# The v projection of an attention block as a sixth pair of seven products, turned to tokens afterwards

## The chip, the cores and the metric

The kernel runs on one core of one Trainium2 chip. The metric is the device time of one execution, in microseconds (us). All arithmetic is in 32-bit floats.

## The reference, cut to what matters

The input x has 32 sequences of 64 tokens with 1024 features. Two blocks follow each other, each with a residual: attention on a projection of x that carries a low-rank addition per sequence, and a feed-forward part with two stages of low-rank experts. Only the attention is touched here:

```
c   = x @ W.T + 0.5 * (x @ lora_A[label]) @ lora_B.T      # per sequence, rank 32
qkv = c @ w_qkv.T + b_qkv                                 # 1024 q, 256 k, 256 v columns
q, k, v = split(qkv)         # 32 query heads, 8 key/value heads of 32
q, k = rope(q), rope(k)
s   = q @ k.T / sqrt(32), causal within the 64 tokens
x   = x + (softmax(s) @ v) @ w_o.T + b_o
```

## The kernel before, in words

The 2048 tokens are taken in two halves of 1024 (the loop over `hf`, which begins at line 897). Ahead of the loop the weights are multiplied out once: `cqkv` is w_qkv times W, so that q, k and v come from x in one product, and `b1q` holds the matching low-rank rows. x lies with features on the partitions (eight tiles of 128 x 1024).

*A pair by seven products.* Large products are made as 2x2 blocks by seven block products in place of eight (class `Group`, lines 231 to 339). A pair is 256 output features. `weight_sums` (line 172) makes four sums of its weights on GpSimd, lines 179 to 182; `column_sums` (line 185) makes four sums of the right side on VectorE, lines 191 to 197. The sums of x, `xt`, are made once per half in four tiles of 128 x 4 x 512, `sum0` to `sum3` (`all_column_sums`, line 224). A step, for example `p1`, is four matmuls of 128 x 128 by 512 columns, all recorded at line 261: p1 uses the plain weights and x, p5 uses weight sum 1 and `sum0`, p6 weight sum 2 and `sum1`, p7 weight sum 3 and `sum2`, p4 `sum3`, p3 weight sum 4, p2 plain operands. p6 and p7 end in a VectorE addition (lines 288 and 300), p1 in a ScalarE copy (line 282). `RankGroup` (line 375) adds the low-rank rows as matmuls with 32 contraction rows (line 385), [...]; the row of the last block is held back to the next pair (`last_rows`, `held`).

*q and k* are five such pairs (`qk_pair`, line 950). Their results get bias and rope: a shuffle, two products and a sum, on VectorE and GpSimd (lines 937 to 948).

*v* is made otherwise. For each of eight blocks of 128 tokens, `v_mult` (line 988) runs eight matmuls with a block of x as the stationary side and 256 columns of weights as the moving side, so that v comes out with tokens on the partitions, as the softmax needs it. `v_ranks` (line 975) adds the low-rank rows at line 979 and `v_out` (line 999) the bias. The weights are loaded by `load_w` at the end of the fifth pair.

*Softmax by units.* A unit is four sequences of one group of four key/value heads; there are eight units in a half. `scores` (1004) makes four banks of scores on TensorE; `masked` (1030) adds the mask on VectorE into tiles `e`; `maxima` (1039) takes the row maxima on VectorE and subtracts them on GpSimd (line 1044); `normalised` (1046) takes exponentials on ScalarE (1048), sums and reciprocals on VectorE (1053, 1054) and multiplies on GpSimd (1056); `turned` (1058) transposes each `e` on TensorE into a bank `pt` (line 1064) and copies it on ScalarE to `ws` (1066); `values` (1070) multiplies with v (1079) and copies two banks to q's place on ScalarE (1087). Banks come from two rings of PSUM: five of `ps_tile`, three of `group_bank`.

*The order* of the stage is written out by hand (`with tc.manual_schedule()` from line 1177), on all engines: every engine takes its instructions in the order in which the program names them. Units 0 and 1 begin in the last two q pairs. Then, in the stage around the change (lines 1212 to 1233):

```
for u in range(4):
    ws = turned(u)
    if u > 0: normalised(u + 1)
    v_mult(2u+1); v_out; masked(u + 2)
    v_ranks; v_mult(2u+2); maxima(u + 2); v_out
    values(u, ws)
```

so each unit's values follow its transposes after one or two v products. The column sums of the output projection, `o_sums` (line 1131), are made from two units at a time on VectorE between them. Units 4 to 7 are then worked between the steps of the output projection's pairs (lines 1239 to 1269).

Of the kernel before, what the change touches and what calls it, by code (L numbers as in the profile page):

```python
# [13 lines left out]
F32 = mybir.dt.float32  # L14
# [5 lines left out]
P = 128  # L20
D = 1024
KC = D // P
B, S = 32, 64
T = B * S
HD, NH, NKV = 32, 32, 8
# [15 lines left out]
for _name, _w in (  # L41
    ("ident", P),
    ("cos", S),
    ("sin", S),
    ("mask", S),
    ("parts", 2 * E),
    ("stack", P),
    ("em8", E),
    ("row", 1),
    ("biases", 10 + 2 * KC),  # L50
    ("bv", NKV * HD),
):
    _C[_name] = slice(_n, _n + _w)
    _n += _w
# [22 lines left out]
def block_kernel(ctx: ExitStack, tc: tile.TileContext, a, out: bass.AP):  # L77
# [32 lines left out]
    em8, row = cst[:, _C["em8"]], cst[:, _C["row"]]  # L110
    biases, bv = cst[:, _C["biases"]], cst[:, _C["bv"]]

# [20 lines left out]
    for n in (512, 512, 128):  # L133
        nc.tensor.matmul(ps[:, :n], idle[:, :P], idle[:, :n], start=True, stop=True)
    bqk, bo, bb = biases[:, 0:10], biases[:, 10 : 10 + KC], biases[:, 10 + KC :]

# [87 lines left out]
    def all_column_sums(name, pool, b, n):  # L224
        t = columns(name, pool, b, n)
        for j in range(4):
            for kc in range(H):
                t.make(kc, (j,))
        return t
# [145 lines left out]
    class RankGroup(Group):  # L375
# [22 lines left out]
        def together(self, held=None):  # L398
# [6 lines left out]
            if held is not None:  # L405
                held.out01()

        def p4(self):
            self.mult(self.y, "22", "t4")
            self.out(1, 0, self.y, self.add10)  # L410
# [85 lines left out]
    b1q = const.tile([P, NQ], F32, tag="b1q", name="b1q")  # L496
    b1d = const.tile([P, 5, P], F32, tag="b1d", name="b1d")
    b2s = scratch.tile([P, NF], F32, tag="b2s", name="b2s")
# [7 lines left out]
    with tc.tile_pool(name="gen", bufs=1) as gen:  # L506
# [190 lines left out]
        make_cf(1, 2, 3)  # L697
        differences(b1d, b1q, 5)
        b2 = hp.tile([P, TH], F32, tag="hw", name="b2").rearrange("p (k o) -> p k o", o=P)
# [197 lines left out]
    for hf in range(2):  # L897
# [13 lines left out]
        attention, pools = pools, ExitStack()  # L911
        xt = all_column_sums(f"x{hf}", scoped(f"sums_x{hf}"), x_half, 512)
        if hf == 0:
            low = first_pass["low"]
        else:
            low = new_low(hf)
            a1 = q[:, 1].rearrange("p b m t -> p b (m t)")
            tiles = [a1[:, s * BS : (s + 1) * BS] for s in range(NS)]
            steps = [ranks(hf, s, x, tiles[s : s + 1], low) for s in range(NS)]
            first_halves, second_halves, sums = zip(*steps)  # L920
# [29 lines left out]
        def qk_pair(g, z_bank=group_bank):  # L950
# [4 lines left out]
            def out(r, c, ps, add):  # L955
                oc = 2 * g + r
                raw = tmp(f"raw_{hf}_{oc}_{c}")
                bias = bqk[:, oc : oc + 1]
                if add is None:
                    nc.scalar.activation(raw, ps, AF.Identity, bias=bias)  # L960
                else:
                    nc.vector.scalar_tensor_tensor(raw, ps, bias, add, ALU.add, ALU.add)
                rope(oc, c, raw)

# [5 lines left out]

        begun = {}

        def v_ranks(*ts):
            for at, t in enumerate(ts):
                begun[t] = group_bank(f"v_{hf}_{t}")[:, :WG]
                rows = slice(at * LR, (at + 1) * LR)
                nc.tensor.matmul(
                    begun[t],  # L980
                    low[rows, t * P : (t + 1) * P],
                    b1q[rows, 5 * WG :],
                    start=True,
                    stop=False,
                    skip_group_check=True,
                )

        def v_mult(t):
            for kc in range(KC):
                nc.tensor.matmul(  # L990
                    begun[t],
                    x[kc][:, t * P : (t + 1) * P],
                    wv[:, kc, :],
                    start=False,
                    stop=kc == KC - 1,
                    skip_group_check=True,
                )

        def v_out(t):
            nc.vector.tensor_add(v[:, t, :], begun.pop(t), bv)  # L1000

        def scores(u):
            g, b0 = u // 4, u % 4 * 4
            sc = [ps_tile(f"sc_{hf}_{u}_{j}") for j in range(4)]
            for n in range(8):
                mp, b = n // 4, b0 + n % 4
                for j in range(4):
# [47 lines left out]

        def turned(u):

            turned = []  # L1060
            for j, e in enumerate(units.pop(u)):
                pt = ps_tile(f"pt_{hf}_{u}_{j}")
                for n in range(4):
                    nc.tensor.transpose(pt[:, n * P : (n + 1) * P], e[:, n * P : (n + 1) * P], ident)  # L1064
                ws = wsp.tile([P, 512], F32, tag="ws", name=f"ws_{hf}_{u}_{j}")
                nc.scalar.copy(ws, pt)  # L1066
                turned.append(ws)
            return turned

        def values(u, turned, bank=ps_tile):  # L1070
# [3 lines left out]
            for i in range(2):  # L1074
                for j in range(4):
                    for b in range(2):
# [3 lines left out]
                            av[b][j * HD : (j + 1) * HD, i * 256 : (i + 1) * 256],  # L1080
                            v[rows, b0 // 2 + i, head * HD : (head + 1) * HD],
                            turned[j][rows].rearrange("p (m i q) -> p i m q", m=2, i=2)[:, i],
# [3 lines left out]
            for b in range(2):  # L1086
                nc.scalar.copy(
                    q[:, g, b0 + b : b0 + 4 : 2, :, :],
                    av[b].rearrange("p (i m t) -> p i m t", i=2, t=S),
                )  # L1090
# [86 lines left out]
        with tc.manual_schedule():  # L1177
# [3 lines left out]
            for u in range(2):  # L1181
# [16 lines left out]
                else:  # L1198
                    wv = load_w(cqkv[:, :, 5 * WG :], f"v{hf}")
                g.p4()  # L1200
                g.p3()
            g.last_rows()
            v_ranks(0, 1)
            g.out01()
            v_mult(0)
            rotated()
            pools.close()
            wsp = scoped(f"ws{hf}", 4)
            sums = scoped(f"sums_o{hf}")
            t0 = [sums.tile([P, 2, 512], F32, tag=f"sum{j}", name=f"sum{j}_o{hf}0") for j in range(4)]  # L1210
            v_out(0)
            for u in range(4):
                first, second = 2 * u + 1, 2 * u + 2
                ws = turned(u)
                if u > 0:
                    normalised(u + 1)
                v_mult(first)
                v_out(first)
                if 0 < u < 3:
                    o_sums(0, t0, u - 1, u)  # L1220
                masked(u + 2)
                if u == 3:
                    values(u, ws, group_bank)
                    o_sums(0, t0, u - 1, u + 1)
                    maxima(u + 2)
                    break
                v_ranks(second, second + 1)
                v_mult(second)
                maxima(u + 2)
                v_out(second)  # L1230
                values(u, ws)
                if u == 0:
                    wo0 = o_load(0, 0)

            wo1 = o_load(0, 1)
# [3 lines left out]
            for u in range(4, 8):  # L1239
                o = pairs[u - 4]  # L1240
                ws = turned(u)
                o.p1()
# [377 lines left out]
```

## Time and profile before

| what | before |
|---|---|
| three runs | 1198.10, 1198.75, 1201.41 us; median 1198.75 |
| the profiled execution | 1199.29 us, its span 1197.5 us |
| busy in the span | TensorE 1186.4 us, VectorE 695.5, GpSimd 533.5, ScalarE 156.9 |
| v products (line 990) | 256 records, 382 ns each, 58.7 us busy |
| transposes of the units (line 1064) | 256 records, 274 ns each, 31.0 us busy |
| the stage around the change, first half | 429.44 to 482.39 us: TensorE busy 52.95, VectorE 47.2, GpSimd 30.4, ScalarE 19.5 |

The span is the time from the first to the last recorded instruction; the profiled execution's own time is 1.8 us more. PE is TensorE, DVE is VectorE, ACT is ScalarE, POOL is GpSimd, SP is the engine that issues most DMAs, PEld is TensorE's loading of weights. A matmul of 32-bit floats appears as two records, a transpose as one. Matmuls are pipelined, so the duration of one record is longer than the distance to the next; what a group costs is the distance from its start to the start of the next group. In a timeline a row gives start and duration, line, operation, written and read tiles, and in brackets the idle time before it with what released it.

### The profile page before, as it was taken

How to read it: one execution, taken by the hardware profiler on the slowest of the kernel's cores; microseconds unless marked ns; L12 is line 12 of the kernel's file. 1: busy time of each engine (PE TensorE's matmuls, PEld its weight loads, DVE VectorE, ACT ScalarE, POOL GpSimd, SP SyncE). 2: the span in 40 equal slices, each digit the busy share in tenths (PEclk: the TensorE clock that was granted, in tenths of full speed). 3: DMA queues.
4: the chain of work that ended last, by engine and by line, in shares of the span. 5: the costliest groups of instructions: out<-in, count | busy, mean ns of one | idle time of the engine just before them, and what ended most of it. 6: DMA issues, size and time to landing. Idle time of an engine off the chain costs nothing.

```text
span 1197.5 us, 15158 instructions
## 1 busy us (share of the span) xinstructions
PE 1186.4 (99%) x5916; PEld 703.9 (59%) x5916; DVE 695.5 (58%) x1221; ACT 156.9 (13%) x302; POOL 533.5 (45%) x477
## 2 busy tenths in 40 slices
PE   9999999999999999999999999999999999999998
PEld 3444874555444468544458887444468644458887
DVE  4313151619556798764757554555898774657552
ACT  1000100000000214330011000000114430011000
POOL 3341355242442756662804533543756762812231
PEclk9999999999999999999999999999999999999999
DMA  6652754858311120122217665111120222313543
GB/s 246 214 216 87 260 176 145 284 165 285 93 35 36 36 71 4 69 71 83 91 36 217 188 201 180 37 35 36 36 71 2 71 71 71 104 31 108 156 145 102
DMA packets 114679, 136.71 MB, mean 114 GB/s; under 512 B 6576, under 2 KB 92976, under 8 KB 113328
## 3 DMA queue, kind: packets, MB, share of 16 engines
q1 hardware_dynamic: 101120, 111.52, 29.2%
q10 hardware_dynamic: 10800, 15.84, 3.7%
q0 software_dynamic: 2688, 8.39, 2.0%
q8 instruction: 47, 0.77, 0.3%
q14 instruction: 24, 0.20, 0.0%
HBM read 101.02 MB, written 34.71 MB: 113 GB/s over the span
## 4 chain that ended last, share of the span: by engine, by line
PE 98%; DMA 1%; SPq 0%; issue 0%; DVE 0%; ACT 0%
PE qk_y L261 9%; PE o_y L261 7%; PE f_y L261 6%; PE qk_x L261 6%; PE qk_z L261 6%; PE v L990 5%; PE o_x L261 5%; PE o_z L261 5%; PE f_x L261 4%; PE f_z L261 4%; PE cf_y L261 3%; PE cq_y L261 3%; PE sc L1011 3%; PE pt L1064 2%; PE cq_z L261 2%; PE f_z L273 2%
## 5 line engine op out<-in xcount | busy, mean ns | idle before, releaser
L938 POOL TENSOR_TENSOR raw<-raw,consts 128x512 f32<-128x512 f32 x40 | 63.1, 1585 | 104.6 <-DVE t L937 104.6
L1044 POOL TENSOR_TENSOR e<-e,top 128x512 f32<-128x512 f32 x64 | 65.0, 1045 | 57.2 <-DVE top L1043 42.2
L261 PE MATMUL f_y<-s_f,w_f 128*128 128x256 f32 x336 | 82.2, 380 | 0.5 <-DVE f_u L300 0.5
L1056 POOL TENSOR_TENSOR e<-e,tot 128x512 f32<-128x512 f32 x64 | 66.2, 1066 | 27.3 <-DVE tot L1054 27.3
L261 PE MATMUL qk_x<-x,w_qk 128*128 128x512 f32 x160 | 72.5, 595 | 0.7 <-ACT qk_p L282 0.7
L261 PE MATMUL qk_y<-sum_x,s_qk 128*128 128x512 f32 x160 | 72.2, 594 | 0.0
L261 PEld LDWEIGHTS f_y<-s_f,w_f 128*128 128x128 f32 x336 | 63.7, 190 | 9.6 <-DVE f_u L300 0.9
L261 PE MATMUL o_x<-q,w_o 128*128 128x512 f32 x128 | 58.9, 592 | 0.0
L990 PE MATMUL v<-w_v,x 128*128 128x256 f32 x256 | 58.7, 382 | 0.0
L1171 POOL TENSOR_TENSOR x<-x,o_u 128x512 f32<-128x512 f32 x24 | 30.9, 1291 | 54.5 <-DVE o_u L1169 33.2
L261 PEld LDWEIGHTS qk_x<-x,w_qk 128*128 128x128 f32 x160 | 30.1, 190 | 39.5 <-issue 37.9
L990 PEld LDWEIGHTS v<-w_v,x 128*128 128x128 f32 x256 | 47.4, 190 | 8.4 <-issue 2.7
L261 PEld LDWEIGHTS qk_y<-sum_x,s_qk 128*128 128x128 f32 x160 | 30.2, 190 | 37.1 <-issue 36.4
L939 DVE TENSOR_TENSOR t<-t,consts 128x512 f32<-128x512 f32 x40 | 48.7, 1229 | 0.7
L1053 DVE TENSOR_REDUCE tot<-e 128x8 f32<-128x512 f32 x64 | 40.5, 667 | 10.7 <-ACT e L1048 10.4
L1048 ACT ACTIVATE e<-e 128x512 f32<-128x512 f32 x64 | 38.3, 641 | 54.2 <-POOL e L1044 54.2
L1034 DVE TENSOR_TENSOR e<-sc,consts 128x512 f32<-128x512 f32 x64 | 39.7, 677 | 8.8 <-PE sc L1011 8.8
L948 DVE TENSOR_TENSOR q<-raw,t 128x512 f32<-128x512 f32 x32 | 38.4, 1206 | 2.5 <-POOL raw L938 2.3
L1043 DVE TENSOR_REDUCE top<-e 128x8 f32<-128x512 f32 x64 | 39.6, 675 | 0.0
L261 PEld LDWEIGHTS o_x<-q,w_o 128*128 128x128 f32 x128 | 23.7, 190 | 26.8 <-issue 26.8
L1066 ACT COPY ws<-pt 128x512 f32<-128x512 f32 x64 | 33.0, 612 | 41.8 <-PE pt L1064 41.8
L261 PE MATMUL qk_y<-sum_x,w_qk 128*128 128x512 f32 x80 | 37.0, 605 | 0.0
(364 smaller groups left out, 2376.1 us busy)
## 6 DMA issues: line engine op xcount, KB each, us to landing
w_f<-cf SPq DMA_DIRECT2D x28, 512.0 KB, 4.0
w_f<-cf SPq DMA_DIRECT2D x28, 384.0 KB, 7.4
w_qk<-cqkv SPq DMA_DIRECT2D x10, 1024.0 KB, 6.7
x<-in_xT SPq DMA_DIRECT2D x16, 512.0 KB, 7.7
w_o<-in_wo SPq DMA_DIRECT2D x16, 512.0 KB
s_o<-wos SPq DMA_DIRECT2D x16, 512.0 KB, 6.6
outT<-o ACTq DMA_DIRECT2D x20, 256.0 KB, 4.0
cqkv<-cq ACTq DMA_DIRECT2D x16, 256.0 KB, 2.3
```

Source lines behind the costliest of these rows:

```text
L261: self.last = nc.tensor.matmul(ps, self.weights[left][:, kc, :], self.right(right, kc), start=first and kc == 0, stop=kc == self.h - 1, sk ...
L938: nc.gpsimd.tensor_mul(rv, rv, c3)
L939: nc.vector.tensor_mul(t2v, t2v, s3)
L948: nc.vector.tensor_add(*unfinished.pop())
L990: nc.tensor.matmul(begun[t], x[kc][:, t * P : (t + 1) * P], wv[:, kc, :], start=False, stop=kc == KC - 1, skip_group_check=True,)
L1011: nc.tensor.matmul(sc[j][:, n * S : (n + 1) * S], q[rows, g, b, 2 * mp : 2 * mp + 2, :].rearrange("p m t -> p (m t)"), k[rows, g, b, :], s ...
L1034: nc.vector.tensor_add(per_key(e), per_key(sc[j]), mask.unsqueeze(1).to_broadcast([P, 8, S]))
L1043: nc.vector.tensor_reduce(top, ev, AX.X, ALU.max)
L1044: nc.gpsimd.tensor_sub(ev, ev, wide(top))
L1048: nc.scalar.activation(e, e, AF.Exp, scale=SCALE)
L1053: nc.vector.tensor_reduce(tot[:, i], es[i], AX.X, ALU.add)
L1056: nc.gpsimd.tensor_mul(es[i], es[i], wide(tot[:, i]))
```

## The change

v becomes a sixth pair of the same form (`qk_pair(5)`): seven products of 512 columns with four weight sums on GpSimd, using the same sums of x. Its results come with features on the partitions, get their bias from a column of `bqkv`, skip the rope and wait in four tiles `v_blocks`. `v_turned` transposes them to tokens with eight TensorE transposes for each half of the columns, and ScalarE copies the banks to `v`. The order of the tokens in v differs from before, so `scores` takes its sequences in the order 0, 2, 1, 3 and `values` reads v at another place.

The `ws` tiles and the tiles of the output projection's sums no longer have pools of their own: they stand in the places of `sum0` to `sum3` whose last product has run (`in_place_of`). The hand-written order changes: p1 and p5 of the v pair come first, units 0 to 3 are turned between its steps, and the values of units 0 to 3 come in a row after it, when v is complete. `normalised(4)` stands after the values of unit 1 and the first `o_sums`. The fifth unit's masks stand ahead of the values. The constants lose the 256 columns of v's bias, and `b1d` gets a sixth block. The core of the diff:

```diff
-        def v_ranks(*ts):
...
-        def v_mult(t):
...
-        def v_out(t):
...
+        def some(self, *what, held=None):
+
+            for at, (r, c) in enumerate(what):
+                self.rows(self.z if c == 1 else self.y if r == 1 else self.x, r, c, at)
+            if held is not None:
+                held.last_rows()
...
+        def in_place_of(j, name):
+
+            return xt.pool.tile([P, 4, 512], F32, tag=f"sum{j - 1}", name=f"{name}_{hf}")
...
-                rope(oc, c, raw)
+                if g == 5:
+                    v_blocks[r, c] = raw
+                else:
+                    rope(oc, c, raw)
...
+        v_blocks = {}
+
+        def v_turned(c):
+            for two in range(2):
+                ps = group_bank(f"v_{hf}_{c}_{two}")
+                for n in range(4):
+                    i, r = 2 * two + n // 2, n % 2
+                    nc.tensor.transpose(
+                        ps[:, n * P : (n + 1) * P], v_blocks[r, c][:, i * P : (i + 1) * P], ident
+                    )
+                at = 4 * c + 2 * two
+                nc.scalar.copy(v[:, at : at + 2, :].rearrange("p t o -> p (t o)"), ps)
...
+        ORDER = (0, 2, 1, 3)
...
-                mp, b = n // 4, b0 + n % 4
+                mp, b = n // 4, b0 + ORDER[n % 4]
...
-                ws = wsp.tile([P, 512], F32, tag="ws", name=f"ws_{hf}_{u}_{j}")
+                ws = to[:, j]
...
-                            v[rows, b0 // 2 + i, head * HD : (head + 1) * HD],
+                            v[rows, 4 * i + b0 // 4, head * HD : (head + 1) * HD],
...
-                    wv = load_w(cqkv[:, :, 5 * WG :], f"v{hf}")
+                    held, pair = g, qk_pair(5)
                 g.p4()
                 g.p3()
-            g.last_rows()
-            v_ranks(0, 1)
...
+            g, ws = pair, {}
+            g.p1()
+            g.p5()
+            ws[0] = turned(0, in_place_of(1, "ws0"))
+            g.some((0, 0), (1, 1), held=held)
+            held.out01()
+            g.p6()
+            masked(2)
+            maxima(2)
+            ws[1] = turned(1, in_place_of(2, "ws1"))
+            rotated()
+            normalised(2)
+            g.p7()
+            g.out11()
+            masked(3)
+            g.p2()
+            g.out(0, 0, g.x, None)
+            maxima(3)
+            g.some((1, 0), (0, 1))
+            wo0 = o_load(0, 0)
+            ws[2] = turned(2, in_place_of(3, "ws2"))
+            g.p4()
+            masked(4)
+            normalised(3)
+            g.p3()
             g.out01()
-            v_mult(0)
...
+            maxima(4)
+            v_turned(0)
+            ws[3] = turned(3, in_place_of(4, "ws3"))
+            v_turned(1)
+            masked(5)
             for u in range(4):
...
+                values(u, ws[u], group_bank if u in (0, 3) else ps_tile)
+                if u == 1:
+                    two = [in_place_of(j, f"sums_o{j}") for j in (1, 2)]
+                    t0 = [t[:, 2 * i : 2 * i + 2] for t in two for i in range(2)]
+                    o_sums(0, t0, 0, 2)
+                    normalised(4)
+            o_sums(0, t0, 2, 4)
+            maxima(5)
...
-                ws = turned(u)
+                ws = turned(u, in_place_of(3 + u % 2, f"ws{u}"))
                 o.p1()
```

More of the change, by code (lines that the diff above doesn't have):

```diff
@@ L49 @@
     ("row", 1),
-    ("biases", 10 + 2 * KC),
-    ("bv", NKV * HD),
+    ("biases", 12 + 2 * KC),
 ):
@@ L110, in block_kernel @@
     em8, row = cst[:, _C["em8"]], cst[:, _C["row"]]
-    biases, bv = cst[:, _C["biases"]], cst[:, _C["bv"]]
+    biases = cst[:, _C["biases"]]
     index = const.tile([P, B + B // 2], I32, tag="index", name="index")
@@ L134, in block_kernel @@
         nc.tensor.matmul(ps[:, :n], idle[:, :P], idle[:, :n], start=True, stop=True)
-    bqk, bo, bb = biases[:, 0:10], biases[:, 10 : 10 + KC], biases[:, 10 + KC :]
+    bqkv, bo, bb = biases[:, 0:12], biases[:, 12 : 12 + KC], biases[:, 12 + KC :]
     lab = const.tile([P, B], F32, tag="lab", name="lab")
@@ L225, in all_column_sums @@
         t = columns(name, pool, b, n)
+        t.pool = pool
         for j in range(4):
@@ L496, in block_kernel @@
     b1q = const.tile([P, NQ], F32, tag="b1q", name="b1q")
-    b1d = const.tile([P, 5, P], F32, tag="b1d", name="b1d")
+    b1d = const.tile([P, 6, P], F32, tag="b1d", name="b1d")
     b2s = scratch.tile([P, NF], F32, tag="b2s", name="b2s")
@@ L697, in block_kernel @@
         make_cf(1, 2, 3)
-        differences(b1d, b1q, 5)
+        differences(b1d, b1q, 6)
         b2 = hp.tile([P, TH], F32, tag="hw", name="b2").rearrange("p (k o) -> p k o", o=P)
@@ L957, in out @@
                 raw = tmp(f"raw_{hf}_{oc}_{c}")
-                bias = bqk[:, oc : oc + 1]
+                bias = bqkv[:, oc : oc + 1]
                 if add is None:
@@ L969, in qk_pair @@
             return RankGroup(f"qk{hf}{g}", w, weight_sums(w, f"qk{hf}{g}"), xt, out, rank, z_bank)
-        begun = {}
-        def v_ranks(*ts):
[L976 to L986, printed above, removed]
-        def v_mult(t):
[L989 to L997, printed above, removed]
-        def v_out(t):
-            nc.vector.tensor_add(v[:, t, :], begun.pop(t), bv)
+        v_blocks = {}
[10 more added lines that the diff above has]
+        ORDER = (0, 2, 1, 3)
         def scores(u):
@@ L1056, in normalised, with turned @@
                     nc.gpsimd.tensor_mul(es[i], es[i], wide(tot[:, i]))
-        def turned(u):
+        def turned(u, to):
             turned = []
@@ L1087, in values @@
                 nc.scalar.copy(
-                    q[:, g, b0 + b : b0 + 4 : 2, :, :],
+                    q[:, g, b0 + 2 * b : b0 + 2 * b + 2, :, :],
                     av[b].rearrange("p (i m t) -> p i m t", i=2, t=S),
@@ L1198, in block_kernel @@
                 else:
-                    wv = load_w(cqkv[:, :, 5 * WG :], f"v{hf}")
+                    held, pair = g, qk_pair(5)
                 g.p4()
                 g.p3()
-            g.last_rows()
-            v_ranks(0, 1)
-            g.out01()
-            v_mult(0)
[L1206 to L1210, printed above, removed]
@@ L1211, in block_kernel @@
-            v_out(0)
-            for u in range(4):
-                first, second = 2 * u + 1, 2 * u + 2
-                ws = turned(u)
[L1215 to L1233, printed above, removed]
+            g, ws = pair, {}
@@ L1240, in block_kernel @@
                 o = pairs[u - 4]
-                ws = turned(u)
+                ws = turned(u, in_place_of(3 + u % 2, f"ws{u}"))
                 o.p1()
@@ L1574 @@
     rows = [_by_member(wqkv[:D]), wqkv[D:]]
-    bias = np.concatenate([_by_member(bqkv[:D]), bqkv[D : D + 256], n(L0_attn_b_o), n(L0_ffn_b_base)])
+    bias = np.concatenate([_by_member(bqkv[:D]), bqkv[D:], n(L0_attn_b_o), n(L0_ffn_b_base)])
     arrays = {
         "consts": np.concatenate(
-            [constants()[:, : _C["biases"].start], bias.reshape(-1, P).T, np.tile(bqkv[D + 256 :], (P, 1))], 1
+            [constants()[:, : _C["biases"].start], bias.reshape(-1, P).T], 1
         ),
```

## The prediction, made before the changed kernel was run

> **What bounds the kernel now.** I read the page first, then the waits of TensorE, then the timelines of the engines in the stage that is rewritten.
>
> ```profile
> span 1197.5 us, 15158 instructions
> ...
> PE 1186.4 (99%) x5916; PEld 703.9 (59%) x5916; DVE 695.5 (58%) x1221; ACT 156.9 (13%) x302; POOL 533.5 (45%) x477
> ...
> PEclk9999999999999999999999999999999999999999
> ...
> PE 98%; DMA 1%; SPq 0%; issue 0%; DVE 0%; ACT 0%
> ```
>
> TensorE is busy for 99% of the span at full clock and is 98% of the chain that ended last. So removed TensorE work shortens the kernel one for one, and every wait that is put in front of TensorE lengthens it one for one. The waits that exist (engine and line waiting, releaser: us in total, times, longest) are elsewhere:
>
> ```profile
> PE h L458 <- issue: 1.8, 1, 1.8
> PE idle L134 <- DVE idle L131: 1.5, 1, 1.5
> ```
>
> None of the eight rows of that view lies in the stage concerned. Its timeline on TensorE in the first half (start, us, instruction; a product is recorded as two) has no gap:
>
> ```profile
> 425.91 3.60 PE L261 MATMUL qk_z<-x,s_qk 128*128 128x512 f32 x8
> 429.45 0.69 PE L979 MATMUL v<-b1q,low 32*128 32x256 f32 x2
> ...
> 430.94 3.72 PE L990 MATMUL v<-w_v,x 128*128 128x256 f32 x16
> 434.50 1.91 PE L1064 MATMUL pt<-consts,e 128*128 128x128 f32 x16
> ...
> 452.74 2.01 PE L1011 MATMUL sc<-k,q 32*128 32x64 f32 x64
> ...
> 477.62 2.01 PE L1011 MATMUL sc<-k,q 32*128 32x64 f32 x64
> 479.57 1.09 PE L1079 MATMUL av<-ws,v 64*32 64x256 f32 x32
> 480.59 1.97 PE L1064 MATMUL pt<-consts,e 128*128 128x128 f32 x16
> 482.39 1.88 PE L261 MATMUL o_x<-q,w_o 128*128 128x512 f32 x4
> ```
>
> The stage runs from the end of the last q/k product (429.44) to the first output-projection product (482.39): 52.95 us; each start minus the one before it is what a group costs. The second half repeats it (its end, from the transposes on, is at 932.43 and 934.23). Its helpers, from the timelines of GpSimd, VectorE and ScalarE:
>
> ```profile
> 431.10 1.78 POOL L938 TENSOR_TENSOR raw<-raw,consts 128x512 f32<-128x512 f32 x1 [2.05 <-DVE t L937]
> ...
> 477.73 4.05 POOL L1056 TENSOR_TENSOR e<-e,tot 128x512 f32<-128x512 f32 x4 [0.24 <-DVE tot L1054]
> ```
>
> ```profile
> 454.31 0.86 DVE L191 TENSOR_TENSOR sum_o<-q 128x256 f32<-128x256 f32 x1
> 455.21 1.15 DVE L193 TENSOR_TENSOR sum_o<-q,sum_o 128x256 f32<-128x256 f32 x1
> ...
> 477.33 0.25 DVE L1054 RECIPROCAL tot<-tot 128x16 f32<-128x16 f32 x1
> 477.50 1.37 DVE L1053 TENSOR_REDUCE tot<-e 128x8 f32<-128x512 f32 x2
> ...
> 479.66 2.48 DVE L1034 TENSOR_TENSOR e<-sc,consts 128x512 f32<-128x512 f32 x4 [0.21 <-PE sc L1011]
> 482.06 0.68 DVE L191 TENSOR_TENSOR sum_o<-q 128x512 f32<-128x512 f32 x1
> ```
>
> ```profile
> 480.75 1.07 ACT L1087 COPY q<-av 128x512 f32<-128x512 f32 x2 [2.59 <-PE av L1079]
> ```
>
> Read here: GpSimd needs 4.05 us for the four multiplications of a unit, 1.01 each, and 1.78 for a rope product beside VectorE; VectorE needs 2.48 for four masks, 1.25 for two sums, 0.17 from start to start for a reciprocal; the strided 128x512 sums for the output projection start 0.61 apart (four make 2.5).
>
> [...] the sums at 454.31 and 455.21, half the width, took 0.86 and 1.15 while GpSimd multiplied, against 0.41 alone at 457.46. [...] the longest gap is 1.8 us.
>
> **The change part by part**, per half.
>
> (1) TensorE work. Out go eight v products of 3.55 (430.94 to 434.50), 28.4, and the low-rank rows: 1.50, 1.09, 0.58 and 0.59, 3.8 in all, one qk row among them. In come seven products of four 512-wide matmuls at 3.43 (322.62 to 326.05 in the same timeline), 24.0, with about 0.1 for entering four of them after small matmuls, 24.4; two row groups at 1.07 (339.88 to 340.95), 2.1; sixteen 128-wide transposes at 1.74/16, 1.7. That is 32.2 against 28.2: 4.0 saved (3.8 to 4.2), 8.0 in both halves. The transposes, scores and values of the units stay the same instructions (1.8, 1.83 and 1.03 a group). This is work on the path, so it counts fully.
>
> (2) Wait before p5 of the v pair. Its first weight sum stands on GpSimd behind the rope product of 431.10, which ends at 432.88. A weight sum takes 1.27 to 1.72 (the row at 401.42), so it lands at 434.2 to 434.7. TensorE ends p1, begun at 429.44, at 432.87. Before, v needed no weight sums. Wait 1.2 to 2.0; I take 1.6.
>
> (3) Turning units 1 and 2, and the second row group: the transposes of unit 1 come straight after four scores and need banks that VectorE's masks release. The fifth bank is free, the others come 0.61 apart. 0 to 0.8, I take 0.5 with the row group's wait for its VectorE result.
>
> (4) Turning unit 3. In the changed order VectorE makes unit 3's sums after the masks of unit 4. From the end of unit 4's scores: masks 2.6, two sums and reciprocal 1.5, first multiplication 1.05, semaphores about 0.1: 5.2. TensorE has p3 (3.43) and half the v transposes (0.87) in between: 4.3. So 0.9 for the first bank, then three times 1.01 - 0.44 = 0.57: 2.6 (2.0 to 3.0). Before, the unit's sums came ahead of a v product and the masks.
>
> (5) Turning unit 4, the largest. After the values of unit 1 the order is: ScalarE copies them out (1.07 and 0.15 to start, the row at 480.75), then exponentials of unit 4 (2.2, beside VectorE); VectorE first makes four sums over units 0 and 1 (2.5), which wait for these copies, then two sums and a reciprocal (1.5); then GpSimd's first multiplication (1.05). 1.2 + 2.5 + 1.5 + 1.05 + 0.2 for semaphores = 6.4. TensorE has only the values of units 2 and 3, 2.05, since the four units' values now stand in a row: wait 4.4. The three further banks follow GpSimd, 0.57 each, 1.7, and VectorE makes the second four sums at that time [...]: 0 to 1.2, I take 0.6. Together 6.7 (5.8 to 7.5). Queued behind these transposes on TensorE is p1 of the output projection and everything after it; nothing later gives this back, since TensorE is full to the end. Before, the exponentials and multiplications of unit 4 ran beside a v product, and the multiplications of 477.73 ended just in time for the transposes of 480.59.
>
> (6) Without price: ScalarE gains a copy, a biased copy and four copies of v (about 3.7), VectorE loses eight additions (0.39 each) and gains two sums and three biased sums (3.6), GpSimd gains four weight sums; where they meet TensorE is in (2) to (5). SP still loads 1 MB for v at the same place, and the first output weights replace the last q/k pair's, free at 429.44 and wanted at 482; the second replace the v pair's, free some 30 us before unit 6 wants them; landing takes 6.7 us in the page. If that cover went, a late load would cost its few us once. The sixth difference row and the smaller constants lie at 300 us and at the start beside full TensorE work. The reused sum places are free when taken: their products precede.
>
> Sum per half: waits 1.6 + 0.5 + 2.6 + 6.7 = 11.4, less 4.0: 7.4 longer. Both halves: 14.8. The profiled execution took 1199.29 (span 1197.5), so 1214.1; the median is 0.54 below it, so about 1213.5.
>
> **The rivals.** (A) Waits are covered and the saved work decides: all four chains of (2) to (5) would have to fit their cover; the deciding point is 4.0 of waits per half. Price: 1198.75 - 8.0 = 1190.8. For it: the same helpers keep pace before, and VectorE's and GpSimd's shares of the span are 58% and 45%. Against it: (5) alone is more, and it is a chain of dependent steps, all with measured durations; the share is an average. 5%. (B) Only (5) bites, at its low end, because VectorE and GpSimd run ahead more than I read: 5.8 - 4.0 = 1.8, +3.6: about 1202.5. For it: (2) and (4) rest on small differences between two long chains. 8%, a quarter of it within 0.3%. (C) The 4.4 us gap also halves TensorE's clock [...]: about 1217. [...] against: [...] GpSimd paces the transposes after it anyway. 10%. My forecast: 77%.
>
> **Numbers.** The low ends of the waits (1.2, 0, 2.0, 5.8 = 9.0, less 4.2) give +9.6, the high ends (2.0, 0.8, 3.0, 7.5 = 13.3, less 3.8) +19.0: 1208.4 to 1217.8. With (C) inside and (B) and (A) left out, 1207.5 to 1218.5. About 0.3% is what a measurement of this kernel can tell from no change: faster 0.05, within it 0.02, slower 0.93.
>
> **What would show it.** In the profile after: no v product of 256 columns; a TensorE wait on GpSimd's weight sum of about 1.6 twice, on the e tiles at the transposes, longest about 4.4 and twice; the stage near 60.4 instead of 52.95; the clock row at 9 throughout, or lower just after the gap under (C). Wrong if the transposes of unit 4 follow the values without a gap, or if new waits appear in the output projection, or if the seven products cost more than 3.43 each.

## The result, and the profile after

| | before | after |
|---|---|---|
| median of four runs each | 1199.7 us (1198.10 to 1201.41) | 1218.95 us (1218.52 to 1220.17) |
| ratio after to before | | 1.016, 95% interval 1.0146 to 1.0173 |
| the profiled execution, its span | 1199.29 us, 1197.5 us | 1219.04 us, 1217.2 us |
| end of the last q/k product to the scores behind the first output product, half 1 / half 2 | 54.77 / 54.79 us | 64.44 / 64.77 us |

The kernel became 1.6% slower (the runs of before are the three known already and one of 1200.65). The forecast, 1213.5 us, had the direction and was 5.5 us short; the time lies 0.45 us above the upper end of the range. Some 0.95 of the 5.5 us is the starting point: the median of before was 1198.75 us for the forecast and is 1199.7 with the fourth run. The rest is growth that was not forecast. The last row of the table is the measure that I use from here on. It starts where the last q/k product ends (429.44 us before, 430.92 after) and ends where the four scores behind the first output product begin, so that it takes in one step more than the forecast's 52.95 us. The two halves of it grew by 9.67 and 9.98 us, 19.65 together, and the span grew by 19.7: all of the loss lies in the rewritten stage.

The page of the changed kernel first. Line 1 is the span, then the busy times, then the granted TensorE clock in 40 slices, then the chain that ended last by engine.

```profile
span 1217.2 us, 14928 instructions
...
PE 1188.5 (98%) x5788; PEld 682.8 (56%) x5788; DVE 705.6 (58%) x1207; ACT 165.0 (14%) x314; POOL 543.0 (45%) x485
...
PEclk9999999999999999899999999999999899999999
...
PE 89%; DVE 5%; POOL 2%; issue 1%; DMA 1%; ACT 0%; SPq 0%; POOLq 0%; DVEq 0%; ACTq 0%
```

TensorE has 128 records fewer and is still busy for 2.1 us longer, although work was taken out: something stretched it. The clock row, all nines before, has two eights, one in each half, and the chain that ended last now runs for 5% on VectorE and 2% on GpSimd. The waits of TensorE name the place (line that waits, releaser: us in total, times, longest):

```profile
PE pt L1065 <- POOL e L1057: 14.1, 14, 4.6
PE qk_z L261 <- POOL s_qk L178: 3.3, 2, 1.7
```

Neither row was there before. The timeline of TensorE in the first half of the changed kernel:

```profile
430.92 3.60 PE L261 MATMUL qk_x<-x,w_qk 128*128 128x512 f32 x8
436.16 3.70 PE L261 MATMUL qk_z<-sum_x,s_qk 128*128 128x512 f32 x8 [1.65 <-POOL s_qk L178]
...
449.01 1.59 PE L1065 MATMUL pt<-consts,e 128*128 128x128 f32 x12 [0.18 <-DVE e L1035]
...
473.23 0.66 PE L1065 MATMUL pt<-consts,e 128*128 128x128 f32 x4 [0.78 <-POOL e L1057]
...
488.24 2.11 PE L1065 MATMUL pt<-consts,e 128*128 128x128 f32 x8 [4.55 <-POOL e L1057]
...
492.13 1.12 PE L1065 MATMUL pt<-consts,e 128*128 128x128 f32 x4 [0.34 <-POOL e L1057]
493.04 2.39 PE L261 MATMUL o_x<-q,w_o 128*128 128x512 f32 x4
495.36 2.01 PE L1012 MATMUL sc<-k,q 32*128 32x64 f32 x64
```

The number in brackets is the wait ahead of a row. Four places have one: p5 of the v pair 1.65 us, the transposes of unit 1 0.18 (on VectorE's masks), the transposes of unit 3 0.78 (its three other banks 0.34 each), the transposes of unit 4 4.55 (later banks 0.33 each). Two durations are unusual for their kind: a bank of unit 4's transposes took 0.9 us (493.04 - 492.13) where unit 3's last took 0.49 (476.23 to 476.72 in the same timeline), and the first output product took 2.39 where the same product had 1.88 before. These two rows lie at the first eight of the clock row. Taken in short stretches, the granted clock of this profile is 1.00 until 487.0, inside the gap, 0.50 from 487.5 to 494.0 and 1.00 again from 495.4: TensorE ran at half its clock there.

The chain of waits of the changed kernel, over the gap ahead of unit 4 (start, us, what):

```profile
480.83 1.06 ACT q L1088 x2
...
482.90 0.70 DVE sums_o L190
...
485.52 1.20 DVE tot L1054 x2
...
487.14 1.32 POOL e L1057 x2
```

It is the chain of step (5), link by link: ScalarE's copies of the values, the first of four output sums on VectorE (the three others follow to 485.52), the sums of unit 4, GpSimd's first multiplications, and only then the transposes. The two helpers of the last part, from the timelines of GpSimd and VectorE:

```profile
487.14 4.94 POOL L1057 TENSOR_TENSOR e<-e,tot 128x512 f32<-128x512 f32 x4 [6.96 <-DVE tot L1055]
```

```profile
484.24 0.68 DVE L194 TENSOR_TENSOR sums_o<-q 128x512 f32<-128x512 f32 x1
...
488.33 1.40 DVE L190 TENSOR_TENSOR sums_o<-q 128x512 f32<-128x512 f32 x1
```

GpSimd's four multiplications took 4.94 us here, and 4.04 for unit 3 in the same timeline. VectorE's output sums took 1.40 beside them (two more 1.41 and 1.52), and 0.68 four us earlier.

### The profile page after: what moved, and what is told of

The parts are those of the page before. It is cut to its first block, busy times and chain, and to the rows that moved or that the text cites. A ratio compares the mean times of both kernels' runs of the same rounds, so it can differ in the third digit from the quotient of the medians.

```text
span 1217.2 us, 14928 instructions
## 1 busy us (share of the span) xinstructions
PE 1188.5 (98%) x5788; PEld 682.8 (56%) x5788; DVE 705.6 (58%) x1207; ACT 165.0 (14%) x314; POOL 543.0 (45%) x485
## 4 chain that ended last, share of the span: by engine, by line
PE 89%; DVE 5%; POOL 2%; issue 1%; DMA 1%; ACT 0%; SPq 0%; POOLq 0%; DVEq 0%; ACTq 0%
PE qk_y L261 10%; PE o_y L261 7%; PE qk_x L261 6%; PE f_y L261 6%; PE qk_z L261 5%; PE o_x L261 5%; PE o_z L261 5%; PE f_x L261 4%; PE f_z L261 4%; PE cq_y L261 3%; PE cf_y L261 3%; PE sc L1012 3%; PE cq_z L261 2%; PE f_z L273 2%; PE pt L1065 2%; PE cf_z L261 2%
## 5 line engine op out<-in xcount | busy, mean ns | idle before, releaser
L261 PE MATMUL qk_x<-x,w_qk 128*128 128x512 f32 x192 | 87.1, 595 | 0.7 <-ACT qk_p L282 0.7
L261 PE MATMUL qk_y<-sum_x,s_qk 128*128 128x512 f32 x192 | 86.9, 595 | 0.7 <-DVE qk_u L288 0.7
L261 PEld LDWEIGHTS qk_x<-x,w_qk 128*128 128x128 f32 x192 | 36.0, 190 | 46.3 <-issue 44.6
L261 PEld LDWEIGHTS qk_y<-sum_x,s_qk 128*128 128x128 f32 x192 | 35.8, 190 | 45.4 <-issue 42.1
L1065 PE MATMUL pt<-consts,e 128*128 128x128 f32 x256 | 37.6, 296 | 14.4 <-POOL e L1057 14.1
L261 PE MATMUL qk_z<-sum_x,s_qk 128*128 128x512 f32 x96 | 43.6, 596 | 3.3 <-POOL s_qk L178 3.3
L1065 PEld LDWEIGHTS pt<-consts,e 128*128 128x128 f32 x256 | 30.4, 150 | 26.0 <-POOL e L1057 20.6
L261 PE MATMUL qk_y<-sum_x,w_qk 128*128 128x512 f32 x96 | 44.2, 603 | 0.0
L261 PE MATMUL qk_z<-x,s_qk 128*128 128x512 f32 x96 | 43.4, 594 | 0.0
```

The lines of the kernel that those rows point to most:

```text
L261: self.last = nc.tensor.matmul(ps, self.weights[left][:, kc, :], self.right(right, kc), start=first and kc == 0, stop=kc == self.h - 1, sk ...
```

## The experiments

All kernels are the changed kernel with an edit. "Stage" is the measure from above, half 1 / half 2, from each run's profile (changed kernel: 64.44 / 64.77 us). Ratios are to the kernel before, run in turns on the same chip (changed kernel: 1.016).

### Unit 4's multiplications ahead of the row of values

```diff
             masked(5)
+            normalised(4)
             for u in range(4):
...
                     o_sums(0, t0, 0, 2)
-                    normalised(4)
```

> Edit: in the changed kernel the multiplications of unit 4 on GpSimd, with the two sums and the reciprocal on VectorE ahead of them, are issued before the row of four values groups instead of after the first two and the four output sums. Nothing is added or left out. Theory (the chain values copy, output sums, sums of unit 4, multiplication makes the 4.55 us gap, and the gap also drops TensorE's clock): the four waits of unit 4, 5.6 us a half together, nearly vanish, and so do the 0.5 to 0.8 us by which the first output product was longer; some 4 to 4.6 us a half come off, 1210.5 us (1209 to 1212). Rival (the seven-product form itself is longer than its matmuls tell, and moving instructions only shifts the wait to another place): about 1219, with a new wait of some 4 us elsewhere in the stage.

Measured: 1211.05 us, ratio 1.0095 (1.0077 to 1.0113); stage 60.28 / 62.44. From TensorE's timeline, a row of each half:

```profile
483.60 0.66 PE L1065 MATMUL pt<-consts,e 128*128 128x128 f32 x4 [1.30 <-POOL e L1057]
...
944.75 3.62 PE L261 MATMUL o_x<-q,w_o 128*128 128x512 f32 x4
```

The first wait fell from 4.55 to 1.30 and nothing came up elsewhere, so the rival falls, and the place of the chain in the queues is shown to be the cause. The waits did not vanish as expected: the masks of unit 5 still stand ahead of unit 4's sums on VectorE, and the last banks still come 1.45 apart, because the output sums are again beside GpSimd's multiplications (4.94 us for the four, 1.40 to 1.52 for a sum). In the first half the output product has its usual 1.88; in the second, with the same gap of 1.30, it has 3.62, and the last two banks of transposes took 1.12 and 1.11 where the first half has 0.66: the lengths that the changed kernel's banks have at a granted clock of 0.50 (mean of the whole execution 0.996). The stage is 2.16 longer for it. That was not expected, and I come back to it.

### Unit 3's sums ahead of the masks of unit 4

```diff
             g.p4()
-            masked(4)
             normalised(3)
+            masked(4)
             g.p3()
```

> Edit: in the changed kernel the sums and multiplications of unit 3 are issued ahead of the masks of unit 4 instead of behind them. Nothing is added or left out. Theory (the order on VectorE alone makes the waits of the transposes of unit 3): the 1.8 us of waits and the transposes stretched by them go, about 2.6 us a half, 1213.6 us (1212.5 to 1215), while the 4.55 us wait of unit 4 stays. Rival (the masks of unit 4, now later, hand the delay on to the turning of unit 4): its wait grows from 4.55 to about 6 and the time stays near 1219.

Measured: 1214.04 us, ratio 1.0122 (1.0105 to 1.0139); stage 62.88 / 62.33. TensorE's timeline:

```profile
470.53 1.91 PE L1065 MATMUL pt<-consts,e 128*128 128x128 f32 x16
...
488.60 3.49 PE L261 MATMUL o_x<-q,w_o 128*128 128x512 f32 x4
```

Unit 3's sixteen transposes run through in 1.74 us (470.53 to 472.27) without a wait. From the first to the second group of v transposes it is 2.62 us now (469.65 to 472.27) and was 5.31 (471.41 to 476.72): 2.69 off, as forecast, and the wait of unit 4 stayed at 4.56, so nothing was handed on. The stage fell by less, 1.56 and 2.44, because the output product behind the gap took 3.49 here and 2.39 in the changed kernel: the clock again (mean of the whole execution 0.993, in the changed kernel 0.994).

### The v pair's weight sums earlier

```diff
-                g.together(held)
+                if u == 0:
+                    g.together(held)
+                else:
+                    for at, (ps, r, c) in enumerate(((g.x, 0, 0), (g.y, 1, 0), (g.z, 1, 1))):
+                        g.rows(ps, r, c, at)
+                    held.last_rows()
+                    g.out11()
+                    g.out(0, 0, g.x, None)
+                    v_pair = qk_pair(5)
+                    held.out01()
...
-                    held, pair = g, qk_pair(5)
+                    held, pair = g, v_pair
```

> Edit: in the changed kernel the four weight sums of the v pair are issued before the last output block of the pair ahead of it, whose rope products on GpSimd they stood behind. Nothing is added or left out. Theory (the 1.65 us wait ahead of the fifth product is the place of the weight sum in GpSimd's queue): the wait goes twice, 1.65 to 1.8 us a half, about 1215.4 us (1214.5 to 1216.3). Rival (GpSimd is the bound there, and the rope product that is now later delays the turned k of that pair): a new wait at the transposes or scores, and 1218 or more.

Measured: 1216.3 us, ratio 1.0134 (1.0117 to 1.0151); stage 64.04 / 63.76. p5 follows p1 after 3.43 us (430.43 to 433.86), where it took 5.24 before the edit: the wait and its 1.81 us are gone in both halves, and no wait came in its place. But the stage fell only by 0.40 and 1.01. In the first half the clock fell at the transposes of unit 3 as well: behind waits of 0.34 the last two banks stand in one row of 2.12 us without a wait, and the v transposes behind them took 1.84 us where they take 1.04 (mean granted clock of the execution 0.991). In both halves the clock also took more behind the gap of unit 4 than in the changed kernel: from the first transpose to the scores behind the output product it was 7.41 and 8.35 us, and 7.12 and 7.45 there.

```profile
433.86 3.60 PE L261 MATMUL qk_z<-sum_x,s_qk 128*128 128x512 f32 x8
...
474.74 1.84 PE L994 MATMUL v<-consts,raw 128*128 128x128 f32 x8
```

### The output sums behind unit 4's sums

```diff
-                    o_sums(0, t0, 0, 2)
                     normalised(4)
+                    o_sums(0, t0, 0, 2)
```

> Edit: in the changed kernel the first four output sums on VectorE are issued after the sums of unit 4 instead of ahead of them; both still come after the values of units 0 and 1. Nothing is added or left out. Theory (the output sums, which wait for ScalarE's copies of the values, are the longest part of the gap): the gap ahead of the transposes of unit 4 falls from 4.55 to about 2.5 us, and being shorter than before it may leave the clock alone: 1213.7 us if the slow transposes and the slow first output product of the changed kernel were the clock, 1215.6 if they were not. Rival (ScalarE's copies and exponentials bound unit 4, not VectorE's order): the gap stays above 4 and the time at 1219.

Measured: 1216.17 us, ratio 1.014 (1.0123 to 1.0157); stage 63.49 / 62.61.

```profile
486.53 0.66 PE L1065 MATMUL pt<-consts,e 128*128 128x128 f32 x4 [2.55 <-POOL e L1057]
487.53 1.09 PE L1065 MATMUL pt<-consts,e 128*128 128x128 f32 x4 [0.35 <-POOL e L1057]
```

The gap fell to 2.55, so the sums' 2 us in the chain are shown, and ScalarE is not what bounds the gap of 4.55. By my estimate it comes next: in the changed kernel its exponentials for unit 4 run from 482.73 to 484.95 and VectorE's masks end at 482.27, so that without the sums between them the first reduction waits for the exponentials, and four sums of 2.5 us give back only 2.0. The other half of the expectation failed: the gap is 2.0 us shorter and the clock fell all the same. The banks took 1.09 to 1.12 us from the second on in the first half, 0.91 and 1.11 from the third on in the second, where the first has 0.66, and the output product 3.42 and 2.54 where it has 1.88 (mean granted clock of the execution 0.996).

### Filling the gap

```diff
             o_sums(0, t0, 2, 4)
+            warm = ps_tile(f"warm_{hf}")
+            for n in range(5):
+                nc.tensor.matmul(
+                    warm, ident, x[n][:, :512], start=True, stop=True
+                )
             maxima(5)
```

> Edit: the changed kernel with five further 128x512 matmuls on TensorE, of the identity with input columns, whose result nobody reads, in the gap ahead of the transposes of unit 4. They take about 2.3 us of the 4.55 us gap and remove no wait; the extra work serves only to keep TensorE from standing idle for so long. Theory [...]: the transposes of unit 4 and the first output product take their usual time again, 1.0 to 1.3 us a half come off, about 1216.5 us (1216 to 1217.3), and the clock row shows no 8. Rival (GpSimd's multiplications, [...] pace the transposes, and the clock has no part in it): no change, 1219 us, or some tenths more.

Measured: 1218.12 us, ratio 1.0158 (1.0144 to 1.0171); stage 63.54 / 63.54. The expected 1216 to 1217.3 us was missed, and by the times alone this is not told from no change. The profile tells the clock's part: the mean granted clock of its execution is 1.000, in the changed kernel 0.994, and behind the filler the rows have their usual length.

```profile
483.13 4.56 PE L1246 MATMUL warm<-x,consts 128*128 128x512 f32 x10
487.76 0.66 PE L1065 MATMUL pt<-consts,e 128*128 128x128 f32 x4
...
490.21 0.66 PE L1065 MATMUL pt<-consts,e 128*128 128x128 f32 x4 [0.79 <-POOL e L1057]
...
492.15 1.88 PE L261 MATMUL o_x<-q,w_o 128*128 128x512 f32 x4
493.96 2.01 PE L1012 MATMUL sc<-k,q 32*128 32x64 f32 x64
```

The fillers took 4.6 us where I had reckoned 2.3, just the whole gap: from the row of values to the first transpose it is 8.61 us with and without them. From the first transpose of unit 4 to the scores behind the output product it is 6.20 us in both halves, and was 7.12 and 7.45: the clock cost 0.92 and 1.25 us there. The last banks still come 1.45 apart, with a wait of 0.79 on GpSimd, so GpSimd paces them and not the clock.

### The second output sums behind unit 5's maxima, alone and with the filler

```diff
-            o_sums(0, t0, 2, 4)
             maxima(5)
+            o_sums(0, t0, 2, 4)
             wo1 = o_load(0, 1)
```

> Edit: in the changed kernel the second four output sums on VectorE, which ran beside the multiplications of unit 4 on GpSimd, are issued behind the row maxima of unit 5. Nothing is added or left out. Theory ([...] 4.94 us for the four multiplications instead of 4.05, 1.40 to 1.52 for a sum instead of 0.68): the multiplications take 4.05 again and the last two banks of unit 4 come 1.0 apart instead of 1.45, 0.9 us a half off the stretch from the first transpose of unit 4 to the first output product, about 1217.2 us; the gap of 4.55 us stays, and so does the slow clock behind it. Rival (the slow clock paces those transposes, not GpSimd): the banks stay 1.45 apart, 1219 us.

> Edit: the last edit together with the five filler matmuls (identity with input columns, result unread) in the gap ahead of the transposes of unit 4; the fillers are added work. Theory [...]: fillers alone took the stretch from the first transpose of unit 4 to the end of the first output product from 7.12 and 7.45 us to 6.20; with both edits it comes to about 5.4 in both halves, and the time to 1216 us (1215 to 1217). Rival (the two terms are one: GpSimd waits for TensorE or the clock follows the pacing): no further gain on the fillers alone, 1218 us.

Measured: alone 1216.3 us, ratio 1.0138 (1.0119 to 1.0158), stage 62.81 / 63.96; with the filler 1215.56 us, ratio 1.0131 (1.0114 to 1.0148), stage 62.65 / 62.64. The timeline of GpSimd with the move alone:

```profile
486.65 4.04 POOL L1057 TENSOR_TENSOR e<-e,tot 128x512 f32<-128x512 f32 x4 [6.97 <-DVE tot L1055]
```

The four multiplications took 4.04 us again. The moved sums now run beside unit 5's subtractions on GpSimd, and those took 5.84 us where the changed kernel has 4.05; no wait of TensorE came from it. TensorE with the move alone, in both halves:

```profile
487.74 3.83 PE L1065 MATMUL pt<-consts,e 128*128 128x128 f32 x16 [4.55 <-POOL e L1057]
491.41 1.88 PE L261 MATMUL o_x<-q,w_o 128*128 128x512 f32 x4
493.22 2.01 PE L1012 MATMUL sc<-k,q 32*128 32x64 f32 x64
...
946.21 4.12 PE L1065 MATMUL pt<-consts,e 128*128 128x128 f32 x16 [4.56 <-POOL e L1057]
950.12 2.79 PE L261 MATMUL o_x<-q,w_o 128*128 128x512 f32 x4
952.84 2.01 PE L1012 MATMUL sc<-k,q 32*128 32x64 f32 x64
```

From the first transpose to the scores this is 5.48 and 6.63 us. With the filler as well, TensorE shows:

```profile
486.81 0.66 PE L1065 MATMUL pt<-consts,e 128*128 128x128 f32 x4
...
488.81 0.66 PE L1065 MATMUL pt<-consts,e 128*128 128x128 f32 x4 [0.34 <-POOL e L1057]
...
490.30 1.88 PE L261 MATMUL o_x<-q,w_o 128*128 128x512 f32 x4
492.12 2.01 PE L1012 MATMUL sc<-k,q 32*128 32x64 f32 x64
```

Banks 1.00 apart (the next at 489.81), 5.31 us from the first transpose to the scores in both halves: 0.89 less than with the filler alone. That is the price of the output sums beside the multiplications. So behind the gap there are three terms: the pace of GpSimd, 5.31 less the 3.57 that transposes (1.75) and product (1.82) take alone, 1.74; the sums beside the multiplications, 0.89; the clock, 0.92 and 1.25 with the sums where they were. Both edits together gain more than either, so the rival falls, but that the terms are separate is not shown: with the sums moved, the clock cost only 0.17 and 1.32 (5.48 and 6.63 less 5.31). In the first half the sixteen transposes stand in one row of 3.83 us, where with the filler there are waits of 0.34 for GpSimd between the banks: they were slow, but the pace of GpSimd, 1.00 a bank, hid nearly all of it, and the output product has its usual 1.88.

### Two of the kernels a second time

> Edit: none against the run with unit 4's multiplications early; the same kernel is profiled a second time to see where TensorE's clock falls. In the first profile it fell in the second half only (transposes of unit 4 and first output product, 8.36 us from the first of these transposes to the next scores, against 6.20 in the first half), with the same gap of 1.30 us ahead in both. Theory ([...] where it falls differs from run to run when the pauses are short): another pattern this time, in the first half, in both or in neither, or a clearly different length. Rival (the place in the program decides): 6.20 and 8.36 us again, to within 0.1.

> Edit: none against the run with the v pair's weight sums early; the same kernel is profiled a second time. In the first profile the clock fell behind the 4.56 us gap in both halves, and in the first half it also fell during the transposes of unit 3, ahead of which TensorE had waited 0.79 us and between which 0.34. Theory [...]: behind the 4.56 us gap the clock falls again in both halves, but by another length (7.41 and 8.35 us from the first transpose of unit 4 to the next scores the first time), and the fall at unit 3 is gone or elsewhere. Rival (the place decides): the same places and lengths to within 0.1 us.

One execution each, 1214.08 and 1214.5 us, which is too little for a comparison of times and is not used as one. From the first transpose of unit 4 to the scores, with unit 4's multiplications early, it was 8.36 and 7.87 us (6.20 and 8.36 the first time). In the first half, which had kept its clock before, the output product now reads:

```profile
489.05 3.62 PE L261 MATMUL o_x<-q,w_o 128*128 128x512 f32 x4
```

With the weight sums early it was 7.27 and 8.35 (7.41 and 8.35), and the fall at unit 3 was gone: the v transposes took 1.04. The rival, the place in the program, falls by the first kernel and by unit 3; behind the gap of 4.55 us the lengths hardly moved. Where the pauses are short, whether the clock falls differs from one execution to the next. The four executions measured first with unit 4's multiplications early fit that: 1209.58 and 1210.33 us at a mean granted clock of 1.000 and 0.999, 1211.76 and 1213.80 at 0.996. Behind the gap of 4.55 us the clock fell every time it was profiled without a filler. Four profiles have that gap and the output sums where they were (the changed kernel, unit 3 early, and the weight sums early twice); in their eight halves the stretch was 7.12 to 8.35 us against 6.20 with the filler: 0.9 to 2.15 us, 1.5 in the mean. At the upper end the output product took 3.55 us to the next start in place of 1.82.

### The three moves together, and then the banks of the values

The first three edits at once (the multiplications of unit 4, the sums of unit 3, the weight sums). Then the same, with the banks of the row of values chosen per unit and per bank:

```diff
-            av = [bank(f"av_{hf}_{u}_{b}") for b in range(2)]
+            two = bank if isinstance(bank, tuple) else (bank, bank)
+            av = [two[b](f"av_{hf}_{u}_{b}") for b in range(2)]
...
-                values(u, ws[u], group_bank if u in (0, 3) else ps_tile)
+                values(u, ws[u], ((group_bank, group_bank), (ps_tile, group_bank), (group_bank, group_bank), (ps_tile, ps_tile))[u])
```

> Edit: the changed kernel with three moves at once: the v pair's weight sums earlier on GpSimd, the sums and multiplications of unit 3 ahead of the masks of unit 4, and those of unit 4 ahead of the row of values. Nothing is added or left out. Theory (the loss is a matter of four waits, the seven products themselves save some 3.3 us a half): waits of 1.8, 2.7 and 7.5 us a half go, less what comes back where the moves meet, some 11 us a half: about 1196.5 us (1194 to 1200), a little below the kernel before. Rival (each move only hands the delay on to the next unit, since VectorE and GpSimd are full in this stage): 1207 or more.

> Edit: the three moves together, and the PSUM banks of the row of values chosen for each unit so that the values of a unit do not take a bank that ScalarE has yet to copy out. Nothing is added or left out. Theory: without the moves this would gain nothing; with them the row of values waits less for copies, 0.5 to 1 us a half below the three moves alone: about 1195 us (1193 to 1198). Rival (the copies are no bound there): the same as the three moves alone.

Measured: three moves 1198.04 us, ratio 0.999 (0.9982 to 0.9999), stage 54.07 / 55.40; with the banks 1195.43 us, ratio 0.9967 (0.9954 to 0.998), stage 52.60 / 52.61. The waits of p5, unit 3 and unit 4 are gone with the moves, but a new one stands in the row of values. The masks of unit 5 now follow unit 4's sums on VectorE, and the values of unit 1 want a bank that still holds scores of unit 5. In the second half the same row took 4.48 behind the same wait, 1.33 more, which I read as the clock again (mean of the execution 0.999, in the run below, which has no such row, 1.000):

```profile
476.61 3.15 PE L1080 MATMUL av<-ws,v 64*32 64x256 f32 x94 [1.78 <-DVE e L1035]
...
926.77 4.48 PE L1080 MATMUL av<-ws,v 64*32 64x256 f32 x94 [1.78 <-DVE e L1035]
```

With other banks the row runs through, and the transposes of unit 4 follow it without a wait:

```profile
474.40 4.95 PE L1081 MATMUL av<-ws,v 64*32 64x256 f32 x128
479.28 1.97 PE L1065 MATMUL pt<-consts,e 128*128 128x128 f32 x16
```

This is the kernel that beats both: 0.33% faster than before (0.2 to 0.46%), 2.17 and 2.18 us a half. Both times lie in the expected ranges, though the banks gave more than the expected 0.5 to 1 us a half (1.47 and 2.79, of which the second half had the 1.33 of the slow row to win back). Whether the banks alone would gain nothing, as the expectation says, no run shows. The stage of before had no gap on TensorE to win back, so what is shorter now is TensorE's work: the seven-product form is worth having, and the order was the loss. The last experiment also gives the saved work: 2.17, plus the 0.47 of unit 1 that remain (448.17 to 450.44 in the changed kernel, 1.80 without a wait), plus 0.76 by which the row of values is longer here than four groups of 1.03 (474.40 to 479.28), is 3.4 us a half.

## Why the forecast was short, step by step

| per half, us | forecast | measured (half 1 / half 2) | how |
|---|---|---|---|
| (1) saved TensorE work | -4.0 | -3.4 | remainder of the stage; again from the last experiment |
| (2) p5 of the v pair | 1.6 | 1.8 | weight sums early |
| (3) units 1 and 2 | 0.5 | 0.5 | timeline |
| (4) unit 3 | 2.6 | 2.7 | sums of unit 3 early |
| (5) gap ahead of unit 4 | 4.4 | 4.55 | timeline; two moves |
| (5) pace of GpSimd | 1.7 | 1.74 | fillers and moved sums |
| (5) output sums beside the multiplications | 0.6 | 0.89 | moved sums |
| clock, left to rival (C) | 0 | 0.92 / 1.25 | fillers |
| sum | 7.4 | 9.7 / 10.0 | stage 9.67 / 9.98 |

The waits were right in place, cause and, but for tenths, size. Rivals (A) and (B) fall: all four chains of (2) to (5) bit. Three things make the 4.85 us between 14.8 and 19.65 for both halves. In the table (1) is what the stage leaves over once the other terms are taken off, so that its sum fits by construction; the last experiment gives the same 3.4 by another way.

The step that failed is the treatment of (C): the slow clock behind the gap stood in the sum with nothing. The forecast had it as a case beside its own, at 10% and about 1217 us, 3.5 above its own 1213.5; that price was the author's estimate, and no run before the change showed one. It is no other case: it follows from the gap that the forecast itself counted on, and behind that gap it came in all ten halves profiled without a filler (a granted clock of 0.50 in the changed kernel). It belonged into the sum at some 1.5 us a half, the mean of the eight halves with the output sums where they were; in the profiled execution it was 2.2 of the 4.85, and in one half of the eight 2.15. The argument against it failed. That GpSimd paces the transposes anyway is true (banks 1.45 us apart with the filler, a wait of 0.79 on GpSimd ahead of the later ones), and it hid nearly all of the slow clock in one half of ten (0.17 us, with the output sums moved). In the changed kernel the slow clock lasts beyond them into the output product, which waits for nobody: 2.39 and 2.71 us where it has 1.88. For the same reason the range was too short: above the sum of all high ends of the waits, 1217.8 us, it left 0.7 us for the clock.

The second is term (1): 3.4 and not 4.0, 1.2 in both halves. Products longer than 3.43 us were one of the signs of being wrong that the forecast had named. The products of the v pair that come after rows, scores or transposes took 3.52 to 3.63 from start to start, p5 behind its wait 3.53, and only p1, behind a product, took 3.43; all seven are 24.8, where I had entered 24.4. The v transposes took 0.88 and 0.97 where nothing waits (469.65 to 470.53 and 472.27 to 473.24 with unit 3 early), 1.85 for both groups, not 1.7, and the scores of three units 1.94 and not 1.83, since transposes or products now follow them where rows with 32 contraction rows did. In the timeline of before as much could be read where the values follow (1.95, from 477.62 to 479.57). Against this stand v products that were 28.7 by their distances and not 28.4.

The third is tenths of p5, the gap and the sums beside the multiplications, some 1.5 in both halves. The largest part is these sums, 0.6: three of them lost 0.7 to 0.85 us each beside the multiplications (1.40 to 1.52 in place of 0.68), and the last two banks came 0.45 later each (1.45 in place of 1.00). What holds the two engines up there is not shown. The forecast's 0.6, out of 0 to 1.2, was the author's estimate.

## What to carry to other kernels

On an engine that is full, a change that saves work in it is to be judged by what stands in front of it afterwards: here 3.4 us a half were saved, and the order of the instructions made some 13 us of waits and slow clock. Moving the same instructions, with other banks for one row of values, left 1.2 of these, and the stage came out 2.2 us shorter than before. If a forecast counts on a gap in TensorE, the slower clock behind the gap (here 0.50 behind 4.55 us, worth 0.9 to 2.15 us) belongs into its sum and its range, and is to be looked for in the instructions behind those that wait. Where helpers feed TensorE, follow the whole chain (copy, sums, reciprocal, multiplication) in their queues for each unit, and put what TensorE needs next ahead of what it needs later.

## What the runs showed that was not expected

TensorE's clock also fell behind pauses much shorter than 4.55 us. Read from the lengths of the rows, as above, it fell behind a gap of 2.55 us followed by shorter waits (both halves), behind one of 1.30 us followed by banks of 0.44 us work each 1.0 to 1.45 us (three of four halves), behind one of 1.78 us within the row of values (one of two), and among the banks of unit 3, 1.0 us apart, with no wait over 0.79 (one of eighteen). Behind the wait of 1.65 us ahead of p5, which has full products on both sides, it did not: the granted clock of the changed kernel is 1.00 there in both halves, and p5 took 3.53 or 3.54 us to the next start in the fifteen halves whose rows show it whole. What decides is not shown: no run separates the length of a pause from the work around it. The fillers show the cheap side of it: matmuls that do nothing useful kept the clock up (mean 1.000 and, with the sums moved, 0.999, where without them it was 0.991 to 0.996 in the kernels with that gap) and did not delay the first transpose (8.61 us with and without them), as they ended within the gap; a gain in the median time is not shown for them alone.
